# Layer 0's attention in a four-layer convolution kernel: other products in groups of up to eight at one step of a pair, GELUs at steps 5, 13 and 21

## The chip, the cores and the metric

The kernel runs on one core of one Trainium2 chip. The metric is the time of one execution on the device in microseconds. Three runs of the kernel before took 3689.62, 3683.67 and 3689.40 us, median 3689.4.

## The reference

Input is x of shape (8, 384, 32, 32) in float32. Four layers follow, each added to its own input after a group norm. The change lies in layer 0:

```python
q = _dwproj(x, dw_q, g_q, b_q, pw_q).reshape(B, heads, hd, N)   # 3x3 depthwise, batch norm,
k = _dwproj(x, dw_k, g_k, b_k, pw_k).reshape(B, heads, hd, N)   # exact GELU, 384x384 product
v = _dwproj(x, dw_v, g_v, b_v, pw_v).reshape(B, heads, hd, N)
attn = jax.nn.softmax(jnp.einsum('bhcn,bhcm->bhnm', q, k) * scale, axis=-1)
out = jnp.einsum('bhnm,bhcm->bhcn', attn, v).reshape(B, C, H, W)
out = jnp.einsum('oc,bchw->bohw', w_out, out)
return _bn(out, g_out, b_out)
```

There are 8 images, 8 heads of 48 channels and N = 1024 positions. Layer 1 is a mixture of four experts, layer 2 a depthwise and a pointwise convolution with ternary weights, layer 3 an attention with sampled keys.

## The kernel before

A first stage convolves all images and writes the results for q, k and v to DRAM (`raw`). Batch norm's scales need all images, so attention starts after it. Attention then goes image by image. The eight heads are worked in **pairs**, four to an image, two heads lying in two halves of the partitions. A projected tile of 128 rows holds two heads of 48 rows, and behind each of them 16 rows more that belong to the heads of pair 3. Pairs 0 to 2 use such a tile (`qk`) as it is; the 16-row pieces are gathered by DMAs (`gather_last`, L468) into a tile `ql`, which pair 3 uses.

For each pair the 1024 queries are taken in two **halves** of 512, and for each half the 1024 keys in eight blocks of 128, two blocks to a **step**. So an image has 4 x 2 x 4 = 32 steps, a pair eight. A step is named below by its number in the image, 0 to 31, or by its `kc` (0, 2, 4, 6).

In each step (loop at L703 and after), TensorE makes the scores of the *next* step (`scores`, L646: per block of keys four matmuls in 64-row quadrants into one of two PSUM tiles of 1024 columns), ScalarE takes their exponential into `p`, and TensorE weighs the values with this step's `p` (`weigh`, L664), summing into two PSUM banks `pav`. After the last step of a half VectorE adds the two banks, transposes, divides and transposes back (`normalise`, L613).

Other products are needed besides, on all 128 rows:

- `project` (L562): queries and keys of the next pair. Four per pair for pairs 0 to 2 (two halves for k, then two for q), three matmuls each. `evac` (L72) copies the bank to SBUF, ScalarE and VectorE taking turns.
- `values` (L541): the next image's values, eight per image, copied by VectorE.
- `out_project` (L582): the finished image's output projection, six per image. VectorE copies it, takes statistics and two sums against x, which SyncE loads; SyncE stores it.

They are put on a list `todo` at the start of a half. At certain steps some are taken off the list, so that they stand behind this step's weighing and before the next scores but one. The list is the only thing that sets their place: they are taken in the order in which they were put on. The banks of these products come from a pool of four (`ps_mm`, L62), of which `pav` holds two.

The rule before, at L749 to L752: in the first half of image 0's first pair, two at each step; else up to four at `kc == 2` of each half.

The next image's tiles are made by loads from `raw` (`load_b`) into a pool of five image tiles, as soon as tiles come free. Before use each of the three tiles (v, k, q) goes through GELU in three chunks on ScalarE (`gelu_chunk`, L492). The table `GELUS` (L539) tells at which steps: the exponentials and GELU use different tables of ScalarE, so each group of three chunks brings a load of the one table and later of the other.

Order: ScalarE's instructions stand as written (L679). The tile framework's scheduler orders the other engines by their dependences; SyncE's queue carries loads, stores and gathers in one order. The last image works its pairs in the order 0, 1, 3, 2 (`ORDER`, L686), the others 0 to 3. In the last image there is no next image, and `out_project` of its first half joins the list in pair 2.

Of the kernel before, what the change touches and what calls it, by code (L numbers as in the profile page):

```python
# [15 lines left out]
KC = C // P  # L16
# [36 lines left out]
def tile_kernel(ctx: ExitStack, tc: tile.TileContext, i: dict, out: bass.AP):  # L53
# [10 lines left out]
    def big(name):  # L64
        return ps_big.tile([P, N], F32, tag="big", name=name)

    def bank(name):
        return ps_mm.tile([P, HALF], F32, tag="mm", name=name)
# [142 lines left out]
    def load_b(b):  # L211
        acts[b] = {}
        for v in (0, 1, 2) if b == 0 else (2, 1, 0):
            acts[b][v] = image(f"g{v}_{b}")
            load_image(acts[b][v], raw[v][b])

    with ExitStack() as pa:
# [124 lines left out]
        sts, taps, todo, later, normed = {}, [], {}, list(work), {0}  # L342
# [149 lines left out]
    def gelu_chunk(g, v, c):  # L492
        nc.scalar.activation(
            g[:, c, :], g[:, c, :], AF.Gelu,
            bias=ss0[:, v, 1, c : c + 1], scale=ss0[:, v, 0, c : c + 1],
        )
# [5 lines left out]
    with ExitStack() as pb:  # L502
# [10 lines left out]
        def values_tile(s):  # L513
            t = wb.tile([P, NT8, 2 * NH0, 32], F32, name=f"vt{s}")
            zero = nc.gpsimd.memset(t, 0.0)

            tc.add_manual_dep(
                zero.ins, scales.ins.name, mybir.DependencyInfo(
                    mybir.DependencyClass.Sync, mybir.DependencyReason.DATA
                ), reason="scales first",  # L520
            )
            nc.gpsimd.memset(t[:, :, :, HQ0 : HQ0 + 1], 1.0)
            vts.append(t)
# [12 lines left out]

        GELUS = {s: [(v, c) for c in range(KC)] for v, s in enumerate((9, 13, 17))}  # L539

        def values(b, t):  # L541
            pv = bank(f"pv{b}_{t}")
            for c in range(KC):
                nc.tensor.matmul(
                    pv[:, :C],
                    lhsT=acts[b][2][:, c, t * P : (t + 1) * P],
                    rhs=w_in[2][:, c, :],
                    start=(c == 0),
                    stop=(c == KC - 1),
                )  # L550
            nc.vector.tensor_copy(
                vts[b % 2][:, t, :, :HQ0],
                pv[:, :C].rearrange("p (h d) -> p h d", d=HQ0),
            )

        def fetch(k):

            b, t = divmod(k, 2)
            fetched[b, t] = image(f"f{b}_{t}")
            load_image(fetched[b, t], o_dram[b] if t else x_img[b])  # L560

        def project(b, pr, v, h):  # L562
            if h == 0:
                qks[b, pr, v] = qp.tile([P, N], F32, tag=f"qk{v}", name=f"qk{v}_{b}_{pr}")
                if pr == 0:
                    qks[b, KC, v] = qp.tile(
                        [P, N], F32, tag=f"ql{v}", name=f"ql{v}_{b}", bufs=1
                    )
            pq = bank(f"pq{v}_{b}_{pr}_{h}")
            for c in range(KC):  # L570
                nc.tensor.matmul(  # L571
                    pq,
                    lhsT=w_in[v][:, c, pr * P : (pr + 1) * P],
                    rhs=acts[b][v][:, c, h * HALF : (h + 1) * HALF],
                    start=(c == 0),
                    stop=(c == KC - 1),
                )
            evac(qks[b, pr, v][:, h * HALF : (h + 1) * HALF], pq)
            if h == 1:
                gather_last(qks[b, KC, v], qks[b, pr, v], pr)  # L580

        def out_project(b, m, h, po=None):  # L582
            hs = slice(h * HALF, (h + 1) * HALF)
            xh = op.tile([P, HALF], F32, tag="xh", name=f"xh{b}_{m}_{h}")
            with tc.issue_after(w_last.ins) if b == 0 else nullcontext():
                nc.sync.dma_start(out=xh, in_=x_img[b][:, m, hs])
            po_new = po is None
            if po_new:
                po = bank(f"po{b}_{m}_{h}")
            for c in range(KC if po_new else 0):  # L590
                nc.tensor.matmul(
                    po,
                    lhsT=wo0[:, c, m * P : (m + 1) * P],
                    rhs=atts[b][:, c, hs],
                    start=(c == 0),
                    stop=(c == KC - 1),
                )
            ot = op.tile([P, HALF], F32, tag="ot", name=f"ot{b}_{m}_{h}")
            if b + 1 < B:
                nc.vector.tensor_copy(ot, po)  # L600
            else:
                nc.scalar.copy(ot, po)
            nc.vector.bn_stats(ost[:, m, 2 * b + h, :], ot if po_new else po)
            (nc.sync if b + 1 < B else nc.scalar).dma_start(out=o_dram[b, :, m, hs], in_=ot)
            cross(b, m, h, xh, ot)

        def spare(k, h):


            vf = vts[B % 2].rearrange("p t h d -> p (t h d)")  # L610
            return vf[:, (2 * k + h) * HALF : (2 * k + h + 1) * HALF]
# [76 lines left out]
        NS = 2  # L688
# [5 lines left out]
        todo = [lambda t=t: values(0, t) for t in range(NT8)]  # L694
        todo.pop(0)()

        def scores_of(b, pr, h, kc):
            return [scores(b, pr, h, kc + k) for k in range(NS)]
# [4 lines left out]
        for n, (b, pr, h, kc) in enumerate(steps):  # L703
            if kc == 0:
                if pr == 0 and h == 0:
                    atts[b] = ap_.tile([P, KC, N], F32, tag="att", name=f"att{b}")
                    if b + 1 < B:
                        load_b(b + 1)
                    else:
                        for k in range(3):  # L710
                            fetch(k)
                if b == 0 and pr == 1 and h == 0:
                    values_tile(1)
                if b + 1 == B and pr == 3 and h == 0:
                    for k in range(3, 5):
                        fetch(k)
                if b + 1 == B and pr == 2 and h == 1:
                    todo += [lambda m=m: out_project(B - 1, m, 0) for m in range(KC)]
                if h == 0 and pr + 1 < KC:
                    todo += [  # L720
                        lambda v=v, q=q, b=b, pr=pr: project(b, pr + 1, v, q)
                        for v in (1, 0) for q in range(2)
                    ]
                if pr == 0 and h == 1 and b > 0:
                    todo += [
                        lambda m=m, q=q, b=b: out_project(b - 1, m, q)
                        for m in range(KC) for q in range(2)
                    ]
                if pr == 2 and h == 0 and b + 1 < B:
                    todo += [lambda t=t, b=b: values(b + 1, t) for t in range(NT8)]  # L730
                if pr == 3 and h == 0 and b + 1 < B:
                    todo += [
                        lambda v=v, q=q, b=b: project(b + 1, 0, v, q)
                        for v in (1, 0) for q in range(2)
                    ]
                pav = [bank(f"pav{b}_{pr}_{h}_{k}") for k in range(2)]
            cur = nxt
            if n + 1 < len(steps):
                nxt = scores_of(*steps[n + 1])
            if b + 1 < B:  # L740
                for v, c in GELUS.get(n % (len(steps) // B), ()):
                    gelu_chunk(acts[b + 1][2 - v], 2 - v, c)
            for k in range(NS):
                weigh(b, pr, kc + k, pav, cur[k])
            if b + 1 == B and pr == 2 and h == 0 and kc == NS:
                for k in range(2):
                    nc.vector.transpose(spare(1, k), spare(0, k))

            early = b == 0 and pr == 0 and h == 0  # L749
            if early or kc == NS:  # L750
                for _ in range(min(2 if early else 4, len(todo))):
                    todo.pop(0)()  # L752
            if kc == NT8 - NS:
                turned = normalise(b, pr, h, pav)
# [30 lines left out]
    _, sco, sho = sc_o  # L785
# [51 lines left out]
    with tc.If(redo > 0):  # L837
        with ExitStack() as pb:
# [13 lines left out]
            with tc.For_i(0, B) as bi:  # L852
# [40 lines left out]
                for pr in range(NPAIR0):  # L893
                    qt, kt = qks[0][:, pr, :], qks[1][:, pr, :]
                    for h in range(2):
                        pav = bank(f"pav_e{pr}_{h}")
                        for j, r in enumerate(HR):
                            hd = 2 * pr + j
                            pt = qp.tile([P, NT8, HALF], F32, tag="pt", name=f"pt_e{pr}_{h}_{j}")
                            for qc in range(4):  # L900
                                q0 = h * HALF + qc * P
                                nm = f"_e{pr}_{h}_{j}_{qc}"
                                s = big(f"s{nm}")
# [13 lines left out]
                                for kg in range(2):  # L917
                                    tp = bank(f"tp{nm}_{kg}").rearrange("p (k q) -> p k q", k=4)
                                    for k in range(4):
                                        kc = kg * 4 + k  # L920
# [1046 lines left out]
```

## Time and profile before

The profiled execution took 3684.65 us; its span, from the first to the last instruction, is 3682.8 us.

| stage, us from the span's start | length | PE busy | DVE busy | ACT busy | clock | DMA share |
|---|---|---|---|---|---|---|
| 0 to 403, convolution | 403.0 | 365.1 | 269.5 | 117.2 | 0.94 | 0.70 |
| 403 to 1792, layer 0's attention | 1389.0 | 1384.1 | 424.0 | 653.2 | 1.00 | 0.18 |
| 1792 to 3683, the other layers | 1891.0 | 1820.5 | 1072.0 | 503.3 | 0.98 | 0.13 |

PE is TensorE, DVE VectorE, ACT ScalarE. The clock is the share of TensorE's full clock that was granted. Matmuls are pipelined and their ends are modelled, so a busy PE is not yet a dense one: the starts of the records tell more. A matmul on float32 stands as two records, so `x12` is two products of three matmuls, `x24` four, and one step's scores and weighing have 16 records each. In a timeline the first column is the start, the second the length, and square brackets name idle time before and what ended it.

### The profile page before, as it was taken

The numbers are of one execution on the slowest core, as the hardware profiler recorded it, in microseconds if no ns is written. First come the engines' busy times: TensorE is split into PE (matmuls) and PEld (weight loads), VectorE is DVE, ScalarE is ACT, GpSimd is POOL, SyncE is SP. The second block draws the span as 40 slices with busy tenths as digits, with TensorE's granted clock in tenths as the row PEclk, the third lists the DMA queues.
The fourth block names the chain that finished last, engine by engine and source line by source line (L and its number), as shares of the span: only waits on it lengthen the run. The fifth ranks groups of instructions, "written<-read, shape, count | busy, mean of one in ns | idle before, by whom it ended". The sixth has DMA issues, their size and how long they took to land.

```text
span 3682.8 us, 39040 instructions
## 1 busy us (share of the span) xinstructions
PE 3569.8 (97%) x15605; PEld 1525.8 (41%) x15605; DVE 1765.5 (48%) x2835; ACT 1273.8 (35%) x1524; POOL 196.1 (5%) x162
## 2 busy tenths in 40 slices
PE   7999999999999999999899999999999999999887
PEld 3444333333333333334434444445344444444434
DVE  6776223232323232323437637475663657547563
ACT  2222354545454444544322222323323232322222
POOL 0000100000000000000000010100102010010112
PEclk9999999999999999999999999999999999999898
DMA  6676311111212120212350010010101001010000
GB/s 205 229 253 228 146 55 34 66 42 58 64 37 64 39 77 27 76 27 74 112 218 23 33 52 20 33 54 33 37 20 48 37 33 43 28 52 20 0 35 18
DMA packets 88179, 253.33 MB, mean 69 GB/s; under 512 B 19114, under 2 KB 19706, under 8 KB 87602
## 3 DMA queue, kind: packets, MB, share of 16 engines
q1 hardware_dynamic: 75000, 211.35, 17.3%
q10 hardware_dynamic: 12408, 37.78, 3.0%
q8 instruction: 127, 2.08, 0.2%
q0 software_dynamic: 576, 1.55, 0.1%
q14 instruction: 68, 0.56, 0.0%
HBM read 133.39 MB, written 75.59 MB: 57 GB/s over the span
## 4 chain that ended last, share of the span: by engine, by line
PE 40%; DVE 9%; ACT 1%; DMA 0%; issue 0%; POOL 0%; DVEq 0%; POOLq 0%; ACTq 0%; SPq 0%
PE y L1327 12%; PE ph L1306 8%; DVE y L1402 6%; PE pq L1447 3%; PE pf L1737 3%; PE pw L1410 3%; PE pav L1637 2%; PE s L1621 2%; DVE hd L1292 1%; PE pss L1650 1%; PE pk L1595 1%; PE pv L1604 1%; PE xsb L1581 1%; PE px L1470 1%; DVE off L1517 1%; PE plog L1056 0%
## 5 line engine op out<-in xcount | busy, mean ns | idle before, releaser
L661 ACT ACTIVATE p<-s 128x1024 f32<-128x1024 f32 x512 | 496.4, 1021 | 508.7 <-PE s L654 508.4
L1327 PE MATMUL y<-hd,w_sb 128*128 128x512 f32 x1080 | 490.5, 600 | 3.5 <-DVE hd L1292 3.5
L669 PE MATMUL pav<-p,vt 64*64 64x512 f32 x4096 | 489.1, 590 | 0.0
L1306 PE MATMUL ph<-h,w_sb 128*128 128x512 f32 x1104 | 485.2, 594 | 1.0 <-DMA w_sb<-in_w_dram 0.9
L654 PE MATMUL s<-qk,qk 48*64 48x512 f32 x3072 | 371.9, 597 | 3.3 <-ACT p L661 3.3
L391 PE MATMUL pk<-st,cw_sb 126*126 126x512 f32 x720 | 320.5, 607 | 11.2 <-DMA st<-pad 10.4
L1306 PEld LDWEIGHTS ph<-h,w_sb 128*128 128x128 f32 x1104 | 207.5, 190 | 260.2 <-issue 255.9
L1327 PEld LDWEIGHTS y<-hd,w_sb 128*128 128x128 f32 x1080 | 198.5, 191 | 245.1 <-issue 233.5
L669 PEld LDWEIGHTS pav<-p,vt 64*64 64x64 f32 x4096 | 165.4, 133 | 276.3 <-issue 268.1
L630 DVE COPY ta<-pav 128x512 f32<-128x512 f32 (+1 forms) x65 | 44.2, 682 | 411.1 <-PE pav L669 411.1
L1402 DVE SCALAR_TENSOR_TENSOR y<-h,tap,y 128x961 f32<-128x961 f32 (+1 forms) x192 | 233.5, 1239 | 0.6
L1316 ACT ACTIVATE hd<-ph,b_sb 128x512 f32<-128x512 f32 x180 | 122.8, 682 | 316.0 <-PE ph L1306 316.0
L391 PEld LDWEIGHTS pk<-st,cw_sb 126*126 126x126 f32 x720 | 139.6, 196 | 183.9 <-issue 180.3
L1517 DVE SCALAR_TENSOR_TENSOR off<-q,dw_sb,off 128x225 f32<-128x225 f32 (+3 forms) x432 | 211.9, 546 | 1.6
L654 PEld LDWEIGHTS s<-qk,qk 48*64 48x64 f32 x3072 | 112.7, 133 | 227.0 <-issue 184.1
L78 DVE COPY qk<-pq 128x512 f32<-128x512 f32 x48 | 33.2, 692 | 292.6 <-PE pq L571 292.6
L397 ACT COPY y<-pk 126x512 f32<-126x512 f32 (+1 forms) x136 | 76.1, 584 | 252.5 <-DMA raw<-y 104.0
L1628 ACT ACTIVATE p<-s 128x1024 f32<-128x1024 f32 x96 | 93.3, 1022 | 191.0 <-PE s L1621 190.9
L1292 DVE TENSOR_TENSOR hd<-hd,cb 128x512 f32<-128x512 f32 x180 | 122.2, 684 | 47.9 <-ACT hd L1316 47.7
L1410 PE MATMUL pw<-y,upw 128*128 128x512 f32 x288 | 129.4, 603 | 9.3 <-DVE y L1402 9.3
L1737 PE MATMUL pf<-att,wp_sb 128*128 128x512 f32 x288 | 130.3, 607 | 4.3 <-DVE att L1664 3.8
L571 PE MATMUL pq<-g,wq_sb 128*128 128x512 f32 x288 | 131.0, 605 | 2.3 <-DMA wq_sb<-in_wq_dram 2.3
(292 smaller groups left out, 3830.1 us busy)
## 6 DMA issues: line engine op xcount, KB each, us to landing
g<-raw SPq DMA_DIRECT2D x72, 512.0 KB
st<-pad SPq DMA_DIRECT2D x180, 168.0 KB
raw<-y ACTq DMA_DIRECT2D x171, 168.0 KB
xa<-in_x_dram SPq DMA_DIRECT2D x24, 512.0 KB
xh<-in_x_dram SPq DMA_DIRECT2D x48, 256.0 KB
f<-in_x_dram SPq DMA_DIRECT2D x24, 512.0 KB
f<-o SPq DMA_DIRECT2D x24, 512.0 KB
o<-ot SPq DMA_DIRECT2D x42, 256.0 KB
```

The source lines that it names most:

```text
L391: nc.tensor.matmul(pk[h].rearrange("p (h w) -> p h w", w=W)[: 3 * nch, :, o0 : o0 + c1 - c0], lhsT=lhs, rhs=rhs, start=(k == 0), stop=(k = ...
L571: nc.tensor.matmul(pq, lhsT=w_in[v][:, c, pr * P : (pr + 1) * P], rhs=acts[b][v][:, c, h * HALF : (h + 1) * HALF], start=(c == 0), stop=(c ...
L654: nc.tensor.matmul(s[64 * k : 64 * k + 64, j * HALF : (j + 1) * HALF], lhsT=kt[r, k0 : k0 + 64], rhs=qt[r, h * HALF : (h + 1) * HALF], sta ...
L661: nc.scalar.activation(p, s, AF.Exp, scale=scale)
L669: nc.tensor.matmul(pav[k][64 * j : 64 * j + 64, :], lhsT=vts[b % 2][r, kc, 2 * hd : 2 * hd + 2, :].rearrange("p a b -> p (a b)"), rhs=p[r, ...
L1292: nc.vector.tensor_tensor(hd, hd, state["cb"], ALU.mult)
L1306: nc.tensor.matmul(ph, lhsT=w1[:, e, c, dc * P : (dc + 1) * P], rhs=state["h1"][c], start=(c == 0), stop=(c == KC - 1),)
L1327: nc.tensor.matmul(y, lhsT=w2[:, e, dc, m * P : (m + 1) * P], rhs=state[h, k], start=(k == 0), stop=(k == NE * KC - 1),)
L1402: nc.vector.scalar_tensor_tensor(d, f, tap2[:, c, t : t + 1], d, ALU.mult, ALU.add)
L1410: nc.tensor.matmul(pw[h], lhsT=upw2[:, c, m * P : (m + 1) * P], rhs=y[c][:, hs], start=(c == 0), stop=(c == KC - 1),)
L1517: nc.vector.scalar_tensor_tensor(d, f, dw3[:, t : t + 1], d, ALU.mult, ALU.add)
L1737: nc.tensor.matmul(pf[:, hs], lhsT=wp3[:, pr, m * P : (m + 1) * P], rhs=att[:, pr, hs], start=(pr == 0), stop=(pr == NPAIR3 - 1),)
```

## The change

Two edits, both in the loop described above.

```diff
-        GELUS = {s: [(v, c) for c in range(KC)] for v, s in enumerate((9, 13, 17))}
+        GELUS = {s: [(v, c) for c in range(KC)] for v, s in enumerate((5, 13, 21))}
...
-            if early or kc == NS:
-                for _ in range(min(2 if early else 4, len(todo))):
+            if early or (h == 1 and kc == NS):
+                for _ in range(min(2 if early else 8, len(todo))):
                     todo.pop(0)()
```

Steps 5, 13 and 21 are `kc == 2` of the second half of pairs 0, 1 and 2. The next image's v tile now goes through GELU at step 5 instead of 9, the k tile at 13 as before, the q tile at 21 instead of 17. The list is emptied once per pair, up to eight, where it was emptied twice, up to four each time. For images 1 to 6 this gives: pair 0 four projections and four output projections; pair 1 two output projections and four projections; pair 2 eight values; pair 3 four projections for the next image. Image 0 has two projections in pair 0 and four in pair 1; the last image has eight in pair 0, six in pair 1, none in pair 3 and three output projections in pair 2. The order of pairs in the last image (0, 1, 3, 2) is in both kernels.

## The prediction

> **What bounds the kernel now.** I read the page first, for the engine that is full, and for whether the stage the change touches is on the path that sets the end.
>
> ```profile
> PE 3569.8 (97%) x15605; PEld 1525.8 (41%) x15605; DVE 1765.5 (48%) x2835; ACT 1273.8 (35%) x1524; POOL 196.1 (5%) x162
> PEclk9999999999999999999999999999999999999898
> L661 ACT ACTIVATE p<-s 128x1024 f32<-128x1024 f32 x512 | 496.4, 1021 | 508.7 <-PE s L654 508.4
> L654 PE MATMUL s<-qk,qk 48*64 48x512 f32 x3072 | 371.9, 597 | 3.3 <-ACT p L661 3.3
> ```
>
> TensorE is the bound. In layer 0's attention (403 to 1792 us, by the stage table: PE busy 1384.1 of 1389.0, DVE 424, ACT 653) the exponentials wait for the scores 508.4 us, and the scores wait for an exponential once, 3.3 us. Moving products therefore pays only where TensorE's own stream gets denser, or where that one wait goes. A busy PE in this profile is no proof of density, so I read TensorE's timeline next and took the distance from one step's first score matmul to the next one's. First a step with two products behind it (12 matmul records; each product has three matmuls and each matmul two records):
>
> ```profile
> 446.91 1.90 PE L654 MATMUL s<-qk,qk 48*64 48x512 f32 x16
> 450.45 5.42 PE L571 MATMUL pq<-g,wq_sb 128*128 128x512 f32 x12
> 455.80 1.95 PE L654 MATMUL s<-qk,qk 48*64 48x512 f32 x16
> 459.29 1.90 PE L654 MATMUL s<-qk,qk 48*64 48x512 f32 x16
> ```
>
> Then a plain step, a step with four products, and the step after it:
>
> ```profile
> 613.86 1.90 PE L654 MATMUL s<-qk,qk 48*64 48x512 f32 x16
> 617.30 1.90 PE L654 MATMUL s<-qk,qk 48*64 48x512 f32 x16
> 620.85 10.57 PE L591 MATMUL po<-att,wo_sb 128*128 128x512 f32 x24
> 631.34 1.95 PE L654 MATMUL s<-qk,qk 48*64 48x512 f32 x16
> ```
>
> A plain step takes 617.30 - 613.86 = 3.44. With two products it takes 8.89, the step after it 3.49: they add 5.45 + 0.05 = 5.50. With four it takes 14.04 and again 3.49 after (next scores at 634.83): 10.60 + 0.05 = 10.65. Two groups of two thus cost 11.00, one group of four 10.65: **a group of products has a fixed price of about 0.35 us**, whatever is in it. Weight loads inside a group follow each other every 0.429 us, and 24 x 0.429 = 10.30, which leaves 0.35 from the other side.
>
> Last, the timeline around the one wait of the scores, image 0, pair 1, half 1, where GELUs come but no products are queued:
>
> ```profile
> 493.88 1.28 ACT L493 ACT_TABLE_LOAD   x1
> 495.17 3.50 ACT L493 ACTIVATE g<-g,ss 128x1024 f32<-128x1024 f32 x3
> 498.69 1.28 ACT L661 ACT_TABLE_LOAD   x1
> 499.99 1.94 ACT L661 ACTIVATE p<-s 128x1024 f32<-128x1024 f32 x2
> 501.06 3.69 PE L654 MATMUL s<-qk,qk 48*64 48x512 f32 x16 [3.26 <-ACT p L661]
> 507.43 1.89 PE L654 MATMUL s<-qk,qk 48*64 48x512 f32 x16
> ```
>
> ScalarE gives 6.1 us to two table loads and three GELUs. TensorE has only plain steps to do, runs out and then starts at half pace (3.69 for sixteen records instead of 1.90). From the scores at 494.19 to those at 507.43 pass 13.24 us where two plain steps take 6.87: **6.37 us lost**. The stage table gives a granted clock of 0.80 for 496 to 513 and 1.00 on both sides.
>
> [...] Attention runs 64-row tiles (48*64, 64*64), the products 128*128[...].
>
> **The change, part by part.** Work and instruction counts do not change; only places do. Outside attention each engine's order is as before.
>
> *Fewer groups.* Group count before, beyond the early steps, which keep their rule: image 0 five, images 1 to 6 seven each (pair 3's second half had nothing left), image 7 five: 52. After: image 0 four, images 1 to 6 four each, image 7 three: 31. So 21 groups go: 21 x 0.35 to 0.36 = **-7.5 us**. A product's own time stays.
>
> *GELUs from steps 9, 13, 17 to 5, 13, 21.* After the change every one of these steps has products behind it: two or eight at 5, four or six at 13, eight at 21. A GELU group with products behind it costs little: after the group at 675.19 the next two steps take 3.57 and 3.54 instead of 3.49 and 3.44, so 0.18 us more. Twenty of the 21 groups pay this already; the one of image 0, step 13, pays 6.37 and will pay 0.18: **-6.2 us**. Its cover is four projections, 10.3 us of TensorE over 6.1 of ScalarE. Table loads stay at the same number.
>
> *What could be late for the moved GELUs.* Image tiles are loaded ahead: the three for image 1 were issued by 377 us and the DMA engines are idle from about 397 to 437, before the new first GELU at about 450. Those for image 2 are issued at 475 to 482 before; the new place of pair 2's projections puts them about 25 us later, for a GELU near 620. Nothing.
>
> *Projections for the next pair, now close before their use.* Between the end of a group and the first scores of the next pair lie one score block and one weighing, 3.5 us, as in pair 1 before; the last copy out of PSUM takes 0.69. In DVE's queue only output projections stand before them, 2.70 us of DVE per product against 2.57 of TensorE, as in today's groups of four, and never more than four in a row. Nothing.
>
> *SyncE's queue.* The gather of a pair's leftover rows and the next image loads move behind the new groups, in the same order but for one exchange: chunk loads no longer stand between the two gathers in the same way. Only the last image uses the gathered rows at once. There the scores wait:
>
> ```profile
> 1724.42 0.33 SPq L169 DMA_DIRECT2D f<-in_x_dram  x1
> 1725.25 1.15 SPq L471 DMA_DIRECT2D ql<-qk  x2
> 1729.60 2.06 PE L654 MATMUL s<-ql,ql 48*64 48x512 f32 x16 [1.60 <-DMA ql<-qk]
> ```
>
> A 512 KB load goes just ahead of the gather. After the change the chunk ahead of it is released by the key projections, about 5 us sooner. This wait lies between 0 and 1.6; if the load is not what makes the gather late, nothing is won. A loss is possible too if more loads ran beside it: +1.5 at most, one chunk's time. I take **-0.6**. POOL's order is unchanged.
>
> Sum: -7.5 - 6.2 - 0.6 = **-14.3 us**. The profiled execution took 3684.65 us (span 3682.8), so it would take 3670.3. The runs shown are 3683.67, 3689.40 and 3689.62: two levels 5.8 us apart, the profiled one on the lower. The median 3689.4 lies on the upper, and would become 3675.1. The level of the coming median is not known from here, so I take the mean of the two, 3686.8, less 14.3: **3672.5**.
>
> **The rivals.**
>
> *A: slower; ScalarE keeps PSUM banks.* Of the four banks of that pool two hold the weighing's sums. The third product of a group needs the bank of the first, and that copy is ScalarE's whenever a key projection leads, queued behind the GELUs. In image 0's step 9 (the same pattern: four projections, GELUs first) the copy ends at 474.55 and the third product starts at 474.96: 0.41 us to spare, and no loss (14.04 for that step). After the change the pattern stands in seven places: step 5 of images 1 to 6 and step 13 of image 0. In step 13 of the other images two output projections lead and DVE frees them. To eat the 14.3 us each place must stall 2.0 us, the copy coming 2.4 later than it did; to be slower by 0.2% (7.4 us) it is 3.1 and 3.5. That needs about one table load and two GELUs more than there are. At that point, 7.4 over the mean of the two levels (3686.8): 3694. Nothing in the trace supplies them; at 0.5 us a place it would give 3676.
>
> *B: half of it.* Either the fixed price comes back elsewhere [...], leaving 6.2 to 6.8, or the hole only moves, leaving about 8. Time 3679 to 3680. Against the first: 12 and 24 records show the same price, and 48 in two neighbouring groups of values (11.49 each, against 3.44 + 24 x 0.32) too. Against the second: no GELU step is without products any more.
>
> *C: the change does not do what it says.* If the queue were empty in the second halves, groups would not merge. The built program's order shows eight products in one group (four projections, four output projections) in images 1 to 6, so this has next to no chance. With it: 3687.
>
> **How the numbers follow.** About 0.2% (7.4 us) is what a measurement of this kernel can tell from no change. Forecast (both gains, -12 to -16): 0.80. B: 0.12, half within 0.2%, half beyond. A: 0.04, mostly slower. C and level scatter between the two sets of runs: 0.04. Faster 0.86, same 0.11, slower 0.03. Range: low end, lower level less 16 and some 4 for other runs, 3664; high end, the upper level with only B's gain, 3683.
>
> **What would show it.** Right: TensorE's score records wait for an exponential nowhere; the stage table at about 490 to 510 has clock 1.00; attention is 13 to 16 us shorter and everything later shifts by that; a step with eight products takes 3.44 + 8 x 2.57 + 0.35, that is 24.4 us, and with eight values 19.2. Wrong: idle time of TensorE's projections ended by ScalarE's copies at steps 5 (A), score blocks after a group longer than 0.05 us above plain without GELUs (B), or a layer after attention that changes its own length.

## The result and the profile after

Six runs of the changed kernel have a median of 3669.99 us (3667.5 to 3675.6), six of the kernel before 3688.27 (3683.67 to 3689.62). The ratio is 0.9956, 95% interval 0.9946 to 0.9966: the mean of the runs is 16 us shorter, between 12.5 and 19.9, and the medians lie 18.3 apart. The profiled execution took 3669.89 us, its span 3668.1, 14.7 less than the span before.

Where the time went is read best from attention alone. I measure it in each trace from the first score matmul to the first matmul after attention (`gmean`, L805): 1403.04 us before, 1388.29 after, 14.75 less. (The stage table of before stops at 1792 us, ahead of the last output projections; so its 1389.0 is a shorter stretch.) Nothing outside attention was changed: the convolution took 1.9 us more here and what follows 1.9 less (1872.3 before, 1870.4 after; between 1868.4 and 1874.7 in the other executions below). The 1.5 to 3.5 us by which the runs moved more than 14.75 are not accounted for; the unchanged part varies by more than that.

The page of the changed kernel, the lines that answer to those of before:

```profile
PE 3561.9 (97%) x15605; PEld 1539.7 (42%) x15605; DVE 1766.6 (48%) x2835; ACT 1273.9 (35%) x1524; POOL 195.9 (5%) x162
PEclk9999999999999999999999999999999999999898
L661 ACT ACTIVATE p<-s 128x1024 f32<-128x1024 f32 x512 | 496.6, 1021 | 370.6 <-PE s L654 370.0
L654 PE MATMUL s<-qk,qk 48*64 48x512 f32 x3072 | 370.8, 592 | 0.0
```

The same instructions, the same ScalarE and VectorE time; the idle time before the scores is 0.0 where it was 3.3.

TensorE's timeline in image 1, pair 0, second half (start, length, then what it is): the new group of eight products.

```profile
602.19 1.89 PE L654 MATMUL s<-qk,qk 48*64 48x512 f32 x16
603.91 1.89 PE L669 MATMUL pav<-p,vt 64*64 64x512 f32 x16
605.73 5.42 PE L571 MATMUL pq<-g,wk_sb 128*128 128x512 f32 x12
610.99 5.31 PE L571 MATMUL pq<-g,wq_sb 128*128 128x512 f32 x12
616.14 10.46 PE L591 MATMUL po<-att,wo_sb 128*128 128x512 f32 x24
626.53 1.95 PE L654 MATMUL s<-qk,qk 48*64 48x512 f32 x16
```

The step takes 626.53 - 602.19 = 24.34 us. A plain step and 48 records at 0.429 come to 24.01, so this group pays 0.33, and the step after a group another 0.05, as with 12 or 24 records. Part of it can be seen on the way in: scores to weighing takes 603.91 - 602.19 = 1.72 us, which is four times 0.429, weighing to the first product 605.73 - 603.91 = 1.82.

The place in image 0 where TensorE had run out, step 13, from the same view:

```profile
482.03 1.90 PE L654 MATMUL s<-qk,qk 48*64 48x512 f32 x16
485.57 5.42 PE L571 MATMUL pq<-g,wk_sb 128*128 128x512 f32 x12
490.82 5.31 PE L571 MATMUL pq<-g,wq_sb 128*128 128x512 f32 x12
496.07 1.95 PE L654 MATMUL s<-qk,qk 48*64 48x512 f32 x16
499.64 2.00 PE L654 MATMUL s<-qk,qk 48*64 48x512 f32 x16
```

And the table by stages (length, busy time with counts of PE, PEld, DVE, ACT and POOL, then the granted clock, DMA share, GB/s):

```profile
490.00:512.00 22.00, 22.00 (x163) 7.97 (x165) 5.14 (x8) 10.81 (x12) 0.00 (x0) 1.00 0.50 156
```

The four projections stand over the GELUs, the clock stays at 1.00, and the next steps take 3.57 and 3.54 us, as after any group with GELUs.

The third place is the last image's pair 3, which uses gathered rows at once:

```profile
1712.96 1.95 PE L654 MATMUL s<-qk,qk 48*64 48x512 f32 x16
1716.45 1.95 PE L654 MATMUL s<-ql,ql 48*64 48x512 f32 x14
```

There is no wait any more; the scores come 3.49 us after those before, where it was 5.28.

So 14.75 = 6.2 (the gap of 6.37, less 0.18 for a covered GELU group) + 1.8 (the step with the gather, of which 1.6 were the wait) + 6.75, which over 21 groups is 0.32 each. This account is arithmetic on two traces; the runs below take its terms apart.

### The profile page after: what moved, and what is told of

It is laid out like the page before. It is cut to its first block, busy times and chain, and to the rows that moved or that the text cites. A ratio compares the mean times of both kernels' runs of the same rounds, so it can differ in the third digit from the quotient of the medians.

```text
span 3668.1 us, 39030 instructions
## 1 busy us (share of the span) xinstructions
PE 3561.9 (97%) x15605; PEld 1539.7 (42%) x15605; DVE 1766.6 (48%) x2835; ACT 1273.9 (35%) x1524; POOL 195.9 (5%) x162
## 4 chain that ended last, share of the span: by engine, by line
PE 39%; DVE 10%; ACT 1%; issue 0%; DMA 0%; POOL 0%; DVEq 0%; POOLq 0%; ACTq 0%; SPq 0%
PE y L1327 11%; PE ph L1306 8%; DVE y L1402 6%; PE pq L1447 3%; PE pf L1737 3%; PE pw L1410 3%; PE pav L1637 2%; PE s L1621 2%; DVE hd L1292 1%; PE pss L1650 1%; PE pk L1595 1%; PE pv L1604 1%; PE xsb L1581 1%; DVE off L1517 1%; PE px L1470 0%; PE plog L1056 0%
```

## Experiments

All kernels are compared with the kernel before on their own chip (medians of 3687.5 to 3688.3 us); the length of attention is from one profiled execution each.

| kernel | median us | runs | ratio to before, interval | attention us |
|---|---|---|---|---|
| before | 3688.27 | 6 | | 1403.04 |
| after | 3669.99 | 6 | 0.9956, 0.9946 to 0.9966 | 1388.29 |
| GELU steps alone | 3686.61 | 12 | 1.0001, 0.9992 to 1.0009 | 1401.83 |
| groups alone | 3746.27 | 1 | | 1461.28 |
| gap of image 0 alone | 3682.34 | 21 | 0.9987, 0.9980 to 0.9993 | 1396.03 |
| groups split again | 3673.33 | 5 | 0.9961, 0.9947 to 0.9975 | 1391.03 |
| products in 64-row tiles | 3658.25 | 4 | 0.9925, 0.9910 to 0.9940 | 1375.57 |
| six GELUs at step 5 | 3675.00 | 1 | | 1395.72 |
| load asked for later | 3685.55 | 1 | | 1401.50 |
| two groups per image | 3666.93 | 5 | 0.9946, 0.9932 to 0.9960 | 1381.94 |
| two groups, other GELU steps | 3664.95 | 6 | 0.9937, 0.9923 to 0.9950 | 1380.75 |
| after, again | 3671.48 | 6 | 0.9960, 0.9948 to 0.9973 | 1388.25 |

### One part of the change alone: the GELU steps

```diff
-        GELUS = {... enumerate((9, 13, 17))}
+        GELUS = {... enumerate((5, 13, 21))}
```

> The kernel before with the GELU steps 5, 13, 21 alone; products still in groups of up to four per half. Theory (21 groups fewer at about 0.35 us each, one uncovered GELU group in image 0 at 6.2, one gather at 1.5): neither the number of groups nor the uncovered group at step 13 of image 0 changes, since all four projections of that pair are taken in its first half. No change: within 2 us of the kernel before, and the 13.2 us for two steps is still there. Rival (the place of the GELUs is what gains): most of the gain is here, 10 to 18 us faster.

No change, as the theory had it. TensorE's waits in its attention, whole: the gap is still there (and the gather).

```profile
PE s L654 <- ACT p L661: 3.4, 2, 3.3
PE s L654 <- DMA ql<-qk: 0.9, 1, 0.9
```

From the scores at 496.83 to those at 508.94 pass 12.1 us here, not 13.2: the waiting is 3.26 again, the slow stretch after it shorter (3.41 us at half clock, 6.83 in the kernel before). The kernel below whose load is asked for later has the same gap, and 12.1 us too. The place of the GELUs by itself gains nothing.

### The other part alone: the groups

```diff
-            if early or kc == NS:
-                for _ in range(min(2 if early else 4, len(todo))):
+            if early or (h == 1 and kc == NS):
+                for _ in range(min(2 if early else 8, len(todo))):
```

with the GELUs at 9, 13 and 17.

> The new rule for the products, up to eight once per pair, with the GELU steps left at 9, 13, 17. Theory: steps 9 and 17 have no products now, so 14 groups of GELUs stand uncovered, and each costs what the one of image 0 cost before, 3.5 us of waiting and up to 2.9 at half clock: 14 x 3.5 to 6.2 = 49 to 87 us, against 14.7 won by groups, step 13 and the gather. 34 to 72 us slower, 3722 to 3760. Rival (exponentials ahead in their buffers hide a GELU group, and the one gap before was an accident of image 0): about 8 us faster, 3680.

58.8 us slower than the kernel before in its one run, attention 58.2 longer. Fourteen places look like this one (image 1, step 9; TensorE's timeline):

```profile
648.42 1.90 PE L654 MATMUL s<-qk,qk 48*64 48x512 f32 x16
651.86 1.90 PE L654 MATMUL s<-qk,qk 48*64 48x512 f32 x16
658.74 3.69 PE L654 MATMUL s<-qk,qk 48*64 48x512 f32 x16 [3.26 <-ACT p L661]
665.05 1.89 PE L654 MATMUL s<-qk,qk 48*64 48x512 f32 x16
```

The step with the wait is 3.44 us over a plain one in each of the fourteen. The next step is over by 1.74 to 3.17 in thirteen and by 0.11 in one. Together they make 76.1. Less the 14 x 0.18 that covered GELU groups would cost, that is 73.6; against the kernel after, which differs in nothing but the GELU steps, attention is 73.0 longer.

The loss of the second step is the slow clock: by the trace, TensorE's clock was halved for 3.4 to 6.3 us after the end of the gap in the thirteen and not at all in the one, and each loss is half of that time to within 0.1 us. (In the kernel before the step lost 2.93 us, and the clock was halved for 5.84 us after the end of the gap.)

The two edits of the change are therefore not two gains: the new rule empties the first halves, and without the new steps the GELUs stand there bare. The step list is what lets the rule pay.

### The gap of image 0 alone

In the kernel before, image 0's second and third GELU groups are put where values are queued:

```diff
-                for v, c in GELUS.get(n % (len(steps) // B), ()):
+                for v, c in GELUS.get({13: 1, 17: 13, 21: 17}.get(n, n) if b == 0 else n % (len(steps) // B), ()):
```

> The kernel before with one edit: in image 0 the second and third group of GELUs move from steps 13 and 17 to 17 and 21, where values are queued; nothing else moves. Theory: the uncovered group goes and nothing takes its place: 6.2 us faster, 3682, two steps at that place take 6.9 us instead of 13.2. Rival (the gap or the slow clock moves elsewhere): no change.

The ratio 0.9987 means 4.8 us faster, 2.6 to 7.4; attention is 7.0 shorter, of which 1.0 is the gather (0.6 us of waiting in this trace, 1.6 before). The five scores from 490.07 on start 3.44 us apart. So the gap's cost goes with this edit, 6.0 us of the 6.2 expected, and nothing took its place. In the two other traces with this gap it cost 5.2 instead of 6.4, so over many runs it is probably worth less than 6.

### Groups split again

In the kernel after, groups over four are split over two neighbouring steps; images 0 to 6 only.

```diff
-            if early or (h == 1 and kc == NS):
-                for _ in range(min(2 if early else 8, len(todo))):
+            if early or (h == 1 and kc in ((NS,) if b + 1 == B else (NS, 2 * NS))):
+                for _ in range(min(2 if early else 8 if b + 1 == B else 4, len(todo))):
```

> The kernel after, but each group over four is split in two, up to four at the second step of a pair's second half and up to four at the third; the last image keeps its groups. 19 more groups, with the same products, GELU places and gather. Theory: 19 x 0.36 = 6.8 us slower than the kernel after, 3677. Rival (the price belongs to the products or was never in the groups): as the kernel after, 3670. In the trace each split pair of groups takes 0.3 to 0.4 us more than one group of eight.

A miss in size: attention grew by 2.74 us, not 6.8, and the times of the two kernels are not told apart. The trace says why (the place of the group of eight shown above):

```profile
603.13 1.89 PE L654 MATMUL s<-qk,qk 48*64 48x512 f32 x16
617.17 1.95 PE L654 MATMUL s<-qk,qk 48*64 48x512 f32 x16
620.76 10.57 PE L591 MATMUL po<-att,wo_sb 128*128 128x512 f32 x24
631.26 1.95 PE L654 MATMUL s<-qk,qk 48*64 48x512 f32 x16
```

The two groups take 14.04 and 14.09, each with its price, and the step after them 3.49: 31.62 us over three steps. The unsplit kernel has 24.34, 3.57 and 3.54, together 31.45. The second group pays its price, but it stands exactly where the exponentials come late after GELUs and the table load, and hides those 0.2 us. A group thus costs 0.35 where it hides nothing and 31.62 - 31.45 = 0.17 just behind GELUs; 19 x 0.17 is 3.2, and 2.74 was measured.

### What a group's price is

Each product is made in two 64x64 tiles, for projections, values and output projections alike (all but the last six of attention). The kernel leaves out half of each sum. The edit of the projections, where `QR` holds the slices of rows 0 to 63 and 64 to 127:

```diff
             for c in range(KC):
-                nc.tensor.matmul(
-                    pq,
-                    lhsT=w_in[v][:, c, pr * P : (pr + 1) * P],
-                    rhs=acts[b][v][:, c, h * HALF : (h + 1) * HALF],
...
+                for r in QR:
+                    nc.tensor.matmul(
+                        pq[r, :],
+                        lhsT=w_in[v][r, c, pr * P + r.start : pr * P + r.stop],
+                        rhs=acts[b][v][r, c, h * HALF : (h + 1) * HALF],
...
```

> The kernel after, with projections, values and output projections made in two 64x64 tiles instead of one of 128x128 (each output half from one half of the contraction only; the other half of each sum is left out, so the output is not the reference's). Each product still streams as many columns, so it should take as long; groups, order and waits stay. Theory (the price of a group is the change of tiling mode): the price goes, 36 groups x 0.35 = 12 to 13 us faster than the kernel after, 3657; a step with eight products takes 24.0 instead of 24.35. Rival (the price comes with a new bank, a new operand or the copies): it stays, 3670.

Attention is 12.72 us shorter than in the kernel after, 0.353 for each of its 36 groups (the 31, and five at the start of image 0), and the time falls with it. Columns per product, copies, banks and the order written are the same; the tile is changed, and with it the count of matmuls, six to a product instead of three, two at a time. The end of the group of eight in this kernel:

```profile
604.46 5.48 PE L574 MATMUL pq<-g,wq_sb 64*64 64x512 f32 x24
609.63 10.03 PE L595 MATMUL po<-att,wo_sb 64*64 64x512 f32 x45
619.08 0.65 PE L658 MATMUL s<-qk,qk 48*64 48x512 f32 x2
619.22 0.87 PE L595 MATMUL po<-att,wo_sb 64*64 64x512 f32 x2
619.56 0.59 PE L658 MATMUL s<-qk,qk 48*64 48x512 f32 x2
```

A product takes as long as before: two pass from 604.46 to 609.63, 5.17 us, where the kernel after takes 5.15 (610.99 to 616.14). Scores begin before the last records of the last output projection do. In the kernel after, the first score matmul never starts less than 0.41 us after the last product matmul.

One more thing differs, and the numbers must be read with it: a product in these tiles uses two of the four 64x64 quadrants that scores use (its records start in pairs, those of scores in fours), and scores began while it still had three records to start (619.08, 619.22 and 619.65 above). This moves time from one group to another. In image 1 the last group and the step after it are 1.19 us shorter than in the kernel after, the first group and its two steps 0.57 longer. The image as a whole (from 595.07 to 767.59, in the kernel after from 602.19 to 776.04) is 1.33 shorter, 0.33 for each of its four groups. The way into a group is free of this: from the first weighing matmul to the first product pass 1.83 us in 26 of the 36 groups of the kernel after, and 1.72, with no loss, in the 21 groups here whose records do not mingle. On the way out, a share of the free quadrants in the gain is not excluded.

So the price goes with the change of tile size: the two changes around one group cost 0.35 us here. What TensorE does in a change, no trace shows.

### Banks kept behind GELUs (the prediction's rival A)

```diff
-        GELUS = {s: [(v, c) for c in range(KC)] for v, s in enumerate((5, 13, 21))}
+        GELUS = {5: [(v, c) for v in range(2) for c in range(KC)],
+                 21: [(2, c) for c in range(KC)]}
```

> The kernel after, with the v and the k tile's GELUs together at step 5 (six chunks) and none at step 13. In images 1 to 6 four projections lead the group at step 5, and ScalarE's copy of the first comes 3.5 us later than with three chunks. Theory (rival A of the prediction is real beyond 0.41 us of slack): TensorE waits for that copy 3.1 us in six places, 18.6, and in image 0, with two products of cover, some 3 to 5; less 7 x 0.18 for GELU groups: 20 to 22 us slower than the kernel after, 3691. Rival (banks are not short): 1 us faster.

Slower than the kernel after, but by a third of what was expected: attention is 7.4 us longer. TensorE in image 1:

```profile
604.60 5.42 PE L571 MATMUL pq<-g,wk_sb 128*128 128x512 f32 x12
609.94 1.07 PE L654 MATMUL s<-qk,qk 48*64 48x512 f32 x2
610.94 5.42 PE L571 MATMUL pq<-g,wq_sb 128*128 128x512 f32 x12
616.20 10.46 PE L591 MATMUL po<-att,wo_sb 128*128 128x512 f32 x24
```

ScalarE's copy of the first product ends at 612.82, yet the third product starts at 610.94. VectorE had copied the second by 610.80, so, going by these times, it took the bank of the second. The scheduler had put one matmul of the next scores into the waiting time. Per image that is 1.2 us over the kernel after, not 3.1: TensorE waited for the earlier of the two copies.

In image 0 something else happens. Only two products stand over the six GELUs, none of them waits for a bank, and the next scores wait 1.62 us for an exponential, with the clock staying at full; the step takes 1.7 us more than one with a covered group. Less 0.18 for each of seven GELU groups saved, the sum is 6 x 1.2 + 1.7 - 1.3 = 7.6. The shortage of banks is real, at 1.2 us a place.

### The gather of the last image

> The kernel before, with one image load of the last image asked for two pairs later (with the two that are asked for at the start of its pair 3), so that no chunk of it stands ahead of the last gather in SyncE's queue. Theory: the scores of pair 3 of the last image wait for the gather 0 to 0.3 us instead of 1.6 (0.6 and 0.9 in two other runs with the same queue); the time does not show it. Rival (the gather itself is that slow): the wait stays at 0.6 to 1.6.

```diff
-                        for k in range(3):
+                        for k in range(2):
                             fetch(k)
...
-                    for k in range(3, 5):
+                    for k in range(2, 5):
                         fetch(k)
```

Inconclusive: the scheduler put the load where it had been, in front of the gather, perhaps because its buffer comes free only there. The scores waited 1.21 us:

```profile
1725.36 0.33 SPq L169 DMA_DIRECT2D f<-in_x_dram  x1
1726.19 1.15 SPq L471 DMA_DIRECT2D ql<-qk  x2
1730.14 2.06 PE L654 MATMUL s<-ql,ql 48*64 48x512 f32 x16 [1.21 <-DMA ql<-qk]
```

With that queue the wait was 1.6, 0.9, 0.6 and 1.2 us in four executions, and the scores started 3.4 to 4.4 us after the first DMA of the gather was issued. In six executions with the new rule for the groups the nearest load goes 3.9 us ahead of the gather instead of 0.8, and the scores started without a wait, 2.5 to 2.6 us after that issue. That the chunk ahead of the gather makes the difference is likely and not shown.

### Fewer groups still

The theory says where to go on: two groups per image. Both later pairs' projections are taken in pair 0, behind the output projections; values and the next image's first projections in pair 3.

```diff
-        GELUS = {s: [(v, c) for c in range(KC)] for v, s in enumerate((5, 13, 21))}
+        GELUS = {5: [(v, c) for v in range(2) for c in range(KC)],
+                 29: [(2, c) for c in range(KC)]}
...
-                if h == 0 and pr + 1 < KC:
-                    todo += [
-                        lambda v=v, q=q, b=b, pr=pr: project(b, pr + 1, v, q)
-                        for v in (1, 0) for q in range(2)
-                    ]
+                if b == 0 and h == 0 and pr == 0:
+                    todo += [lambda v=v, q=q: project(0, 1, v, q) for v in (1, 0) for q in range(2)]
...
+                if pr == 0 and h == 1:
+                    todo += [
+                        lambda v=v, q=q, b=b, p2=p2: project(b, p2, v, q)
+                        for p2 in ((2,) if b == 0 else (1, 2)) for v in (1, 0) for q in range(2)
+                    ]
-                if pr == 2 and h == 0 and b + 1 < B:
+                if pr == 3 and h == 0 and b + 1 < B:
                     todo += [lambda t=t, b=b: values(b + 1, t) for t in range(NT8)]
...
-                for _ in range(min(2 if early else 8, len(todo))):
+                for _ in range(min(2 if early else 16, len(todo))):
```

> The kernel after, with two groups per image instead of four: six output projections and then both pairs' eight projections at step 5, eight values and four projections at step 29; GELUs in two groups, v and k tiles at step 5, q tile at 29. 15 groups fewer, x 0.35 = 5.3, seven GELU groups fewer, x 0.18 = 1.3, against about 1.5 to 3 once in image 0, where projections lead behind six GELUs. Theory: 4 to 5 us faster than the kernel after, 3665.5. Rival (longer groups bring stalls of their own: VectorE's 2.70 us per output projection against 2.57 over six in a row, gathers queued behind): same as the kernel after or slower, 3670 to 3675.

Attention is 6.35 us shorter than in the kernel after, more than the 4 to 5 expected. In image 0, where projections lead behind six GELUs, the bank shortage shows as in image 1 of the kernel with six GELUs, and costs 1.2 us. The next form moves three GELUs away from there:

```diff
-        GELUS = {5: [(v, c) for v in range(2) for c in range(KC)],
-                 29: [(2, c) for c in range(KC)]}
+        GELUS = {5: [(0, c) for c in range(KC)],
+                 29: [(v, c) for v in (1, 2) for c in range(KC)]}
```

> The kernel with two groups per image as before, but at step 5 only the v tile's GELUs (three chunks), and at step 29 those of the k and q tiles (six chunks), where eight values, copied by VectorE, lead the group. Theory (what image 0 lost in the other form, 1.2 to 1.7 us, was the bank of a projection kept behind six GELUs): that loss goes, attention is 1.2 to 1.7 us shorter than in the other form and about 7.8 shorter than in the kernel after; 3662 in the time. Rival (six GELUs cost the same wherever they stand): as the other form, 3664 to 3667.

> The kernel after once more, beside the one with two groups on the same chip: 3670, and 14 to 19 us faster than the kernel before. Attention in the trace within 0.5 us of the first profile of it (1388.3 from the first scores to the first product after attention), if the account by groups holds from one execution to the next.

Attention takes 1380.75, 1.2 shorter than in the other form and 7.5 shorter than in the kernel after, whose second profile gave 1388.25 (1388.29 in the first). A group of fourteen products in it:

```profile
600.81 1.90 PE L654 MATMUL s<-qk,qk 48*64 48x512 f32 x16
604.36 15.72 PE L591 MATMUL po<-att,wo_sb 128*128 128x512 f32 x36
635.36 5.31 PE L571 MATMUL pq<-g,wq_sb 128*128 128x512 f32 x12
640.60 1.95 PE L654 MATMUL s<-qk,qk 48*64 48x512 f32 x16
```

The step takes 39.79 us, 0.35 over a plain step and 84 records; six output projections in a row stall nothing. On one chip this kernel took 3664.95, where 3662 was expected, and the kernel after 3671.48. Each of its six runs is shorter than each of the six of the kernel after (at most 3666.32, at least 3669.53), though the intervals to the kernel before (0.9923 to 0.9950, 0.9948 to 0.9973) overlap by 0.0002. The kernel after itself comes out at 0.9960 of the kernel before there, 14.8 us.

## Why the prediction was right

It forecast 14.3 us less, and attention gave 14.75; it put the time at 3672.5 in a range of 3664 to 3683, and it is 3670.0. The mechanism is the forecast one. That the sizes agree so closely is in part luck: the groups gave less and the gather more than was put on them, and the profiled execution of the kernel before has the dearest of that gap's three executions and the longest of the four waits for the gather. Step by step:

- **The bound.** TensorE's density sets attention. Right: attention shrank by what TensorE's stream lost, while ScalarE's and VectorE's work stayed (1273.8 and 1273.9 us, 1765.5 and 1766.6 over the whole).
- **Fewer groups, -7.5.** Right in kind, a little large: 6.75, or 0.32 a group. Merging in the traces shows the price, and the tiles of 64 rows what it goes with. That 48 records pay no more than 24 was only argued from two groups of 24; the kernel after shows it. The eight-product step was to take 24.4 and took 24.34, eight values 19.2 and took 19.22.
- **The gap of image 0, -6.2.** Right, shown by its own experiment at 6.0; but the same gap of 3.26 us cost 5.2 where the clock was halved for half as long, 3.41 us instead of 6.83. In the kernel before the clock fell 2.26 us after the gap began, before its end.
- **The gather, -0.6.** Too small: the wait vanished, 1.6 in the profiled pair (1.8 with its step) and about 1.1 over four executions. The forecast took less than half of an interval from 0 to 1.6 because it could not tell the load's part from the gather's own. (The 1.5 given there for one chunk is an estimate; 512 KB at the 355 GB/s that the DMA view of the kernel before shows near 1727 us come to 1.48.)
- **Things costed at nothing.** Loads for the moved GELUs, the projections close before their use, SyncE's new order: no wait of TensorE's matmuls stands for any of them in attention. Two small losses were not on the list. The steps with pair 3's projections take 14.08 us instead of 14.04, once 14.19, 0.4 in all; from the first weighing matmul to the first product pass 1.87 us there, once 1.97, instead of 1.83, and the trace shows no wait for another engine. The step with the last image's last group takes 11.94 instead of 11.61, for a cause that is open. Together they are the 0.7 us by which the groups fell short of 7.5.
- **Rival A** was given a price of stalls one for one with ScalarE's lateness. Measured, it is 1.2 us for 3.5 of lateness, because the other copy's bank comes first. It did not occur in the changed kernel.
- **Rival B**, a price that comes back after long groups, did not occur: the step after a group without GELUs takes 3.49 as before. **Rival C** neither.
- **The level.** The forecast took two levels of the time for given and went between them. With more runs there are no two levels: 56 runs of the kernel before spread from 3679 to 3693 without a gap of more than 1.7. The middle between the supposed levels was 1.5 below the median that came.

What the prediction did not say is that the two edits hang together. It set down 6.2 for the GELU steps and 7.5 for the groups; alone they are worth nothing and minus 58. The 6.2 do not come from moved GELUs at all: those of step 13 stay where they were, and the new rule brings four projections to them.

## What to carry to other kernels

Where TensorE is full and alternates between tile sizes, count the changes of tile size: each excursion from 64-row to 128-row matmuls and back cost 0.35 us here, with 12 records as with 84, so other work is best gathered into few long groups, as far as banks and copies keep up. Before gathering, list what else those groups were covering; here three GELUs with their two table loads (6.1 us of ScalarE, of which 1.28 for each load) need other TensorE work behind them (two products, 5.1 us, were enough; two under six GELUs were not), and a group taken from them costs 3.5 to 6.6 us, ten times and more what merging wins. Let a group be led by products whose copies the other engine makes: values, copied by VectorE, led behind six GELUs without the loss of 1.2 us that projections had.

## What was not expected of the hardware

- A gap of 3.26 us in TensorE's stream costs more than itself, but not always the same: over the fourteen gaps of the kernel with the groups alone, the step after it lost 1.74 to 3.17 us to the slow clock in thirteen and almost nothing in one. In that trace the clock was halved after a gap for 3.41 us or twice that, beginning 2.1 to 5.0 us after the gap's start, and all its changes lie a whole number of 3.41 us from each other, as they do in the traces of the kernels before and after. How long TensorE must be idle for the clock to fall is open.
- Attention without a gap repeats to 0.05 us between two executions of one kernel (1388.29 and 1388.25), while the unchanged rest varies by 6 us (1868.4 to 1874.7). A difference of a few us in one stage is better read from that stage's trace than from the time.
- Where products and scores had tiles of one size, TensorE began scores 0.14 us before the last records of the product started (lines above), the two in part in different quadrants.
